# Turned attention weights: from an image in DRAM to sixteen transfers a unit within SBUF

## The chip, the cores and the metric

The kernel runs on one core of a Trainium2 chip. The metric is device time in microseconds, the median of several runs. The profile comes from one further execution, taken by the hardware profiler; its engines are TensorE (PE, with PEld for weight loads), VectorE (DVE), ScalarE (ACT), GpSimd (POOL) and SyncE (SP), which issues nearly all DMA transfers here.

## The reference

One transformer block with adaptive layer norm, in float32, for 8 sequences of 1024 tokens and width 512, 16 heads of 32:

```python
mod = jax.nn.silu(condition) @ Wada + bada
sh_a, sc_a, gt_a, sh_m, sc_m, gt_m = jnp.split(mod, 6, axis=1)
xm = _layernorm(x, g1, be1) * (1.0 + sc_a[:, None, :]) + sh_a[:, None, :]
x = x + gt_a[:, None, :] * _attention(xm, Wqkv, Wproj, bproj)
xm = _layernorm(x, g2, be2) * (1.0 + sc_m[:, None, :]) + sh_m[:, None, :]
h = jax.nn.gelu(xm @ W1 + b1, approximate=False)
x = x + gt_m[:, None, :] * (h @ W2 + b2)
```

`_attention` is causal: per head `softmax(where(causal, q @ k.T * 32 ** -0.5, -inf)) @ v`, then the output projection.

## The kernel before

The 8 sequences are cut into 16 blocks of 512 tokens; a sequence's first block (even number n) attends to itself only, its second (odd n) to both. Activations and weights stay in float32. The linear layers (k, q, v, output projection, up, down) go through `matmul` (line 217), four matmuls of 32 rows of output side by side; the square ones are cut into seven products instead of eight, from sums of weight quarters that a preparation leaves in DRAM. Weights come in pieces of 256 KB through a ring of eight SBUF buffers (`fetch`, lines 347 to 363; issues on lines 358, 360, 362): a piece is fetched when the piece eight before it is used up.

All instructions are written out in one order by a planner in the kernel's Python code. `note`, `note_pe` and `note_dma` keep a planned clock for each engine; generators ("threads") yield what they wait for, and `work` advances the one that is due first by that clock. The main thread is the linear work, window by window; the attention's loops put score and weight work between, at a pace (`pace`, `stream`), and side threads started with `start` handle smaller chains. On the chip each engine then works through its own list in order, SP too: an issue that waits holds back all issues behind it. Normalised tiles (`turn`, lines 723 and 728) also pass SP: written to DRAM (`held`) and read back turned (`hat`), and TensorE needs them for the linear layers (`xm_a`, `xm_m`).

Attention works in groups g of four heads (128 of the 512 columns). For the odd blocks and block 0, scores are computed twice, once to find row maxima (line 1613), once transposed (line 1721), so that the exponentials come out with keys in partitions, as the product with v needs them. The other even blocks, n = 2, 4, ..., 14, seven of them, are attended "by rows" (`attend_rows`). There the scores are computed once, with query rows in partitions, in ten units a block (`row_units`, `rows_unit`). A unit takes:

- a page, one of three SBUF buffers of 128 x 2048 (`free_p`, `take_slot`, `give_slot`), at most two of them raw pages at a time (`raws`);
- matmuls into the one score bank `st` (line 2021), a mask (2028), row maxima (2032), and exponentials by ScalarE into the raw page, with the sums accumulated (line 2040);
- one transpose of 32 x 32 squares by VectorE in place (line 2053).

What remains is to bring the squares to their mirrored partitions. Before the change this passes DRAM: `scatter` (line 2068) writes each part of the page into an image, `gather` reads a group's finished image back as three pages of up to eight squares by two key blocks (line 2143), and the products with v run over up to 256 columns at a time into the one bank `po` (line 2155):

```python
(both, 0, 0, 2), (both, 1, 1, 2)                        # page 0 of a group
(both, 0, 2, 2), (second, 1, 3, 3), (first, 1, 1, 1)    # page 1
(both, 0, 0, 0),                                        # page 2
```

Each entry gives the query columns, the place in the page, the key block and the first query block. As long as a block still has units to issue, one page of turned weights is held at a time (`pages`, `PAGE`). `inverses` turns the row sums' reciprocals into a tile of rows through a small DRAM tile (lines 2097 and 2105), and `finish_rows` multiplies the bank with it (line 2183, or 2179 and a multiply). The following odd block's first product waits in the plan until all four groups are `gathered` (line 1925).

## Time and profile before

| | us |
|---|---|
| median of 3 runs | 3542.0 |
| lowest, highest | 3541.5, 3550.18 |
| the profiled execution | 3545.22 |
| its span, first to last instruction | 3543.5 |
| TensorE busy in it | 3377.7 |
| VectorE busy | 2339.5 |
| ScalarE busy | 1248.8 |
| GpSimd busy | 1762.9 |

The DMA engines moved 645.42 MB, 506.31 MB of it read from HBM and 129.27 MB written, counted by the instructions. A busy share is a mean over stages with different limits; the stages attended by rows begin at 416, 818, 1252, 1682, 2111, 2535 and 2963 us. In groups of instructions a line ends with busy time, the mean of one in ns, and the engine's idle time before them with what ended it. A product of the program appears as two matmul instructions.

### The profile page before, as it was taken

The page shows a single profiled execution, that of the slowest core. Times are in us where ns is not written, and L with a number is a line of the kernel's source. Part 1 is how long each engine was busy: PE and PEld are TensorE (multiplying, and loading weights), DVE is VectorE, ACT ScalarE, POOL GpSimd, SP SyncE. Part 2 cuts the span into 40 slices and gives each one's busy share as a digit, 9 for nine tenths or more (in the row PEclk, how much of TensorE's full clock was granted, in tenths as well). Part 3 has the DMA queues.
Part 4 walks back from the last instruction along what each step waited for, and adds up shares of the span by engine and source line. Part 5 has one row for each costly group of instructions (what it writes and reads, how often), then busy time and mean ns, then how long its engine had stood idle before and what let it go on. Part 6 is the DMA issues. An engine that isn't in the chain of part 4 may idle for free.

```text
span 3543.5 us, 118795 instructions
## 1 busy us (share of the span) xinstructions
PE 3377.7 (95%) x52861; PEld 1705.4 (48%) x52861; DVE 2339.5 (66%) x2562; ACT 1248.8 (35%) x1970; POOL 1762.9 (50%) x1710
## 2 busy tenths in 40 slices
PE   8999889999899998999999999999999999899999
PEld 4444445444454444544454454544555445454455
DVE  5766577657577575775767757676677667566563
ACT  2334333343233532335223353333523334232521
POOL 3667713756037650477405674066731667208640
PEclk9999999999999999999999999999999999999999
DMA  6843487537875378753886538865498555973344
GB/s 198 263 148 112 150 235 214 155 109 213 245 209 155 102 226 239 209 153 103 247 233 189 153 109 264 253 185 142 127 284 236 147 142 154 284 221 111 92 135 138
DMA packets 502579, 645.42 MB, mean 182 GB/s; under 512 B 40365, under 2 KB 334061, under 8 KB 498485
## 3 DMA queue, kind: packets, MB, share of 16 engines
q1 hardware_dynamic: 501952, 637.80, 60.8%
q8 instruction: 416, 6.82, 0.8%
q14 instruction: 95, 0.77, 0.1%
q10 hardware_dynamic: 116, 0.03, 0.0%
HBM read 506.31 MB, written 129.27 MB: 179 GB/s over the span
## 4 chain that ended last, share of the span: by engine, by line
PE 37%; DMA 6%; POOL 4%; DVE 3%; issue 1%; SPq 1%; ACT 1%; DVEq 0%; POOLq 0%; ACTq 0%
PE bank L217 27%; PE sc L1613 3%; POOL pT L1856 3%; PE po L1762 2%; PE st L1721 2%; DMA held_m<-xm_m 1%; DMA turned<-image 1%; PE rows_sc L2021 1%; PE st L1709 1%; PE po L2155 1%; DVE mx L1628 1%; DMA w<-in_L_cond_Wproj_dram 1%; DMA hat_m<-held_m 1%; PE bank L1783 0%; DMA w<-in_L_cond_W_dram 0%
## 5 line engine op out<-in xcount | busy, mean ns | idle before, releaser
L1856 POOL TENSOR_TENSOR pT<-pT,pT 128x512 f32<-128x512 f32 (+3 forms) x918 | 981.9, 1104 | 250.5 <-ACT pT L1734 197.2
L217 PE MATMUL bank<-w,hT 128*32 128x256 f32 x14336 | 822.4, 380 | 0.9 <-ACT y_d L204 0.9
L1734 ACT ACTIVATE pT<-st 128x2048 f32<-128x2048 f32 x218 | 409.5, 1879 | 762.1 <-PE st L1721 573.9
L217 PEld LDWEIGHTS bank<-w,hT 128*32 128x32 f32 x14336 | 457.0, 110 | 372.7 <-issue 87.5
L1628 DVE TENSOR_REDUCE mx<-sc 128x4 f32<-128x2048 f32 (+3 forms) x271 | 499.4, 1859 | 183.0 <-PE sc L1613 179.7
L217 PE MATMUL bank<-xm_m,w 128*32 128x256 f32 x8192 | 506.6, 384 | 28.8 <-DMA w<-in_L_cond_W_dram 19.7
L2040 ACT ACTIVATE rows_p<-rows_sc,rows_minus 128x256 f32<-128x256 f32 (+3 forms) x448 | 229.6, 534 | 448.0 <-DVE rows_minus L2034 246.4
L217 PE MATMUL bank<-t_m,w 128*32 128x256 f32 x6144 | 382.9, 380 | 1.1 <-DVE hT L208 0.9
L217 PEld LDWEIGHTS bank<-xm_m,w 128*32 128x32 f32 x8192 | 257.8, 111 | 245.5 <-issue 66.4
L217 PEld LDWEIGHTS bank<-t_m,w 128*32 128x32 f32 x6144 | 190.7, 110 | 179.8 <-issue 58.3
L217 PE MATMUL bank<-xm_a,w 128*32 128x256 f32 x3968 | 252.1, 392 | 26.0 <-DVE xm_a L782 16.3
L217 PE MATMUL bank<-w,qT 128*32 128x512 f32 x2048 | 242.0, 610 | 16.3 <-DMA w<-in_L_cond_Wproj_dram 16.2
L1613 PE MATMUL sc<-kT,qT 32*128 32x512 f32 (+3 forms) x2168 | 250.6, 546 | 6.9 <-DVE mx L1628 3.5
L1762 PE MATMUL po<-pT,v 128*32 128x512 f32 (+3 forms) x2176 | 232.0, 515 | 4.5 <-POOL pT L1739 4.4
L1721 PE MATMUL st<-qT,kT 32*128 32x512 f32 (+3 forms) x2176 | 228.5, 508 | 0.0
L208 DVE TENSOR_TENSOR hT<-bank,u_u 128x512 f32<-128x512 f32 x181 | 121.4, 683 | 113.0 <-PE bank L217 110.6
L217 PEld LDWEIGHTS bank<-xm_a,w 128*32 128x32 f32 x3968 | 131.7, 113 | 131.3 <-issue 29.2
L217 PE MATMUL bank<-t_a,w 128*32 128x256 f32 x2944 | 184.4, 383 | 2.6 <-DVE qT L208 2.1
L2053 DVE STREAM_TRANSPOSE rows_p<-rows_p 128x2048 f32<-128x2048 f32 x70 | 160.9, 2298 | 36.2 <-ACT rows_p L2040 35.5
L1625 DVE TENSOR_TENSOR sc<-sc,mask 128x1024 f32<-128x1024 f32 (+1 forms) x89 | 90.5, 1017 | 124.4 <-PE sc L1613 91.9
L1129 ACT ACTIVATE hT<-hT,cols 128x512 f32<-128x512 f32 x256 | 164.4, 711 | 22.8 <-DVE hT L208 21.6
L655 POOL TENSOR_SCALAR rstd_a<-mv_a 128x4 f32<-128x4 f32 x14 | 3.2, 231 | 333.6 <-DVE mv_a L634 333.1
(268 smaller groups left out, 4152.9 us busy)
## 6 DMA issues: line engine op xcount, KB each, us to landing
w<-in_L_cond_W_dram SPq DMA_DIRECT2D x384, 256.0 KB
w<-kept_up_S SPq DMA_DIRECT2D x256, 256.0 KB
w<-kept_down_S SPq DMA_DIRECT2D x256, 256.0 KB
w<-kept_qkv_S SPq DMA_DIRECT2D x180, 256.0 KB
w<-in_L_cond_Wqkv_dram SPq DMA_DIRECT2D x147, 256.0 KB
image<-rows_p SPq DMA_DIRECT2D x112, 256.0 KB
turned<-image SPq DMA_DIRECT2D x28, 1024.0 KB
turned<-image SPq DMA_DIRECT2D x56, 512.0 KB
```

What stands on the lines that cost most here:

```text
L208: nc.vector.tensor_tensor(out, src, other, op)
L217: nc.tensor.matmul(ps[r, :], columns, rhs, start=start, stop=stop, skip_group_check=True)
L1129: nc.scalar.activation(hT[:, i, :], hT[:, i, :], AF.Gelu, bias=cols[:, O_B1 + f : O_B1 + f + 1])
L1613: nc.tensor.matmul(sc[:, j, c0 : c0 + w], qTs[n][r, gg, ts(qt, P)], keys_of(n, kh)[r, gg, :w], start=True, stop=True, skip_group_check=True,)
L1625: nc.vector.tensor_tensor(place, place, shape_of.to_broadcast(place.shape), ALU.add)
L1628: nc.vector.tensor_reduce(maxima[n, gg][:, kh, qt, :], sc[:, :, c0 : c0 + w], axis=AX.X, op=ALU.max)
L1721: nc.tensor.matmul(st[:, j, c0 : c0 + w], kT[r, gg, ts(k % NTT, P)], qT[r, gg, TB - w :], start=False, stop=True, skip_group_check=True,)
L1734: nc.scalar.activation(pT[:, :, :used], st[:, :, :used], AF.Exp, scale=scale)
L1762: nc.tensor.matmul(po[r, TB - w :], v[:, k % NTT, g * P + j * hd : g * P + (j + 1) * hd], pT[:, j, c0 : c0 + w], start=(k == 0), stop=last ...
L1856: nc.gpsimd.tensor_tensor(into, into, pT[:, j, c0 : c0 + w], ALU.add)
L2040: nc.scalar.activation(tile_of[:, j], sc[:, j, c0 : c0 + w].rearrange("p (k b x) -> p k b x", b=NTT, x=hd), AF.Exp, bias=minus[:, i, j : j ...
L2053: nc.vector.transpose(raw, raw)
```

## The change

The image, its writes and its reads go. When a unit's raw page has been transposed, a thread `spread_unit` takes a second page, and sixteen transfers, one for each pair of partition quarters a and b, move 32 partitions of 512 contiguous elements (64 KB) from the raw page into it; then the raw page is free again. The products with v run from this page over one key block and 128 query columns at a time. Pages are taken in the order of the units, and each unit's products follow those of the unit before. The raw page's columns are laid out in four runs of 512 instead of part by part; the units of a group come in the order of the score units. `finish_rows` no longer waits for the inverses: without them it copies the bank out with ScalarE and multiplies in a thread later. The planned cost of a transfer, and two allowances (1500 and 2500 ns), are new.

```diff
-    SLOT, PAGE = "a page", "a page to turned rows"
-    all_issued, pages = [True], []
+    SLOT = "a page"
...
-            todo += [(g, parts) for parts in mine[2:] + mine[:2]]
+            todo += [(g, parts) for parts in mine]
+        for i, (g, parts) in enumerate(todo):
+            order_of[n, g, parts[0][0]] = i
+            written["paged", n, i] = written["valued rows", n, i] = NEVER
+        written["paged", n, -1] = 0.0
...
-        places, at = [], 0
+        runs = raw.rearrange("p (b r) -> p b r", b=NTT)
         for i, (qt, kh, c0, w, gg) in enumerate(parts):
-            tile_of = raw[:, at : at + HPG * w].rearrange("p (b k j x) -> p j k b x", b=NTT, j=HPG, x=hd)
+            tile_of = runs[:, :, c0 : c0 + w].rearrange("p b (k j x) -> p j k b x", j=HPG, x=hd)
...
             nc.vector.transpose(raw, raw)
             note("DVE", 2320, [("p", slot)], [("p", slot)])
-            start(scatter())
-
-        def scatter():
-            yield [("p", slot)], []
-            for qt, w, gg, at in places:
-                count = w // P
...
-                for a in range(NTT):
-                    into = images[n, gg][qt // 2][:, qt % 2, a, :count, :]
-                    nc.sync.dma_start(
-                        into.rearrange("(b k) s e -> k b (s e)", k=hd),
-                        raw[ts(a, hd), at : at + HPG * w].rearrange("k (b f) -> k b f", b=NTT),
+            written["p", slot] += 1500
+            start(spread_unit(n, raw, slot, parts, order_of[n, g, parts[0][0]]))
...
+    def spread_unit(n, raw, slot, parts, i):
+        while True:
+            yield [("p", slot), SLOT, ("paged", n, i - 1)], []
+            if free_p:
+                break
+        taken_slot = take_slot()
+        key = ("p", taken_slot)
+        yield [("p", slot)], [key]
+        written["paged", n, i] = 0.0
+        page = pp.tile([P, NTT, TB], F32, tag=f"p{taken_slot}", name=f"turned_{n}_{i}")
+        for a in range(NTT):
+            for b in range(NTT):
+                nc.sync.dma_start(page[ts(b, hd), a, :], raw[ts(a, hd), ts(b, TB)])
+                note_dma(190, [("p", slot)], [key])
+        written[key] += 2500
+        left["p", slot] = now["DMA"] + LAND
+        raws.remove(slot)
+        give_slot(slot)
+        if i:
+            yield [("valued rows", n, i - 1)], []
+        for qt, kh, c0, w, gg in parts:
+            first = (n, gg) not in row_outs
+            for k in range(w // P):
+                yield [key, ("v", n), ("v done", n)], ["po"] if first and k == 0 else []
...
+                for j in range(HPG):
+                    r = slice(j * hd, (j + 1) * hd)
+                    at = c0 + k * P + j * hd
+                    nc.tensor.matmul(
+                        out[0][r, ts(qt, P)],
+                        vs[n][:, k, gg * P + j * hd : gg * P + (j + 1) * hd],
+                        page[:, :, at : at + hd],
...
+                note_pe(2 * COLUMN * P, "columns", [key], ["po"])
+            if out[1] == 10:
+                finish_rows(n, gg, out[0])
+        give_slot(taken_slot)
+        written["valued rows", n, i] = 0.0
...
-    def gather(n, g):
...
-            for at, source, ns in moves[i]:
-                nc.sync.dma_start(page[(slice(None), *at)], source)
-                note_dma(ns, [], [key])
-            written[key] += LATE
...
-                    nc.tensor.matmul(
-                        state["out"][r, qt * P : qt * P + wide],
-                        vs[n][:, k, g * P + j * hd : g * P + (j + 1) * hd],
-                        page[:, rows_of, at, r],
...
-            if state["left"] == 0:
-                yield [("inverses", n, g), "po"], []
-                finish_rows(n, g, state["out"])
...
     def finish_rows(n, g, out):
-        key, into, by = ("att", n), qTs[n][:, g, :], inverse_rows.pop((n, g))
-        ready = due(["top", "po"])
-        if max(now["DVE"], ready) > max(now["ACT"], ready) + 2500:
+        into = qTs[n][:, g, :]
+        if wait_of(([("inverses", n, g)], [])) > 0 or max(now["DVE"], due(["po"])) > max(now["ACT"], due(["po"])) + 2500:
             nc.scalar.copy(into, out)
-            note_act(585, None, ["po"], [key])
-            either(into, into, by, ALU.mult, ["top"], [key])
+            note_act(585, None, ["po"], [("values", n, g)])
+            start(scaled(n, g, into))
         else:
-            nc.vector.tensor_tensor(into, out, by, ALU.mult)
+            nc.vector.tensor_tensor(into, out, inverse_rows.pop((n, g)), ALU.mult)
...
+    def scaled(n, g, into):
+        yield [("inverses", n, g), ("values", n, g)], []
+        either(into, into, inverse_rows.pop((n, g)), ALU.mult, ["top"], [("att", n)])
+        finished(n, g)
```

89 lines of the change are left out of this document (13 added, 76 removed).

## The prediction

> **What bounds the kernel now.** I read the page first (engine totals, DMA queue), then the table of stretches over the stages in which seven of the sixteen blocks are attended by rows, the only ones that the change touches. After those came what TensorE waits for, SP's own waits, and the groups and lines that carry the durations.
>
> ```profile
> span 3543.5 us, 118795 instructions
> ...
> PE 3377.7 (95%) x52861; PEld 1705.4 (48%) x52861; DVE 2339.5 (66%) x2562; ACT 1248.8 (35%) x1970; POOL 1762.9 (50%) x1710
> ```
>
> TensorE is busy for 95%, so all its idle time together is 166 us, and no change beside it can win much more than that. The first seven lines below run each from the first row score of such a block to its last product; the eighth is the stage of a block done the other way.
>
> ```profile
> core 0: us, PE busy (x) PEld busy (x) DVE busy (x) ACT busy (x) POOL busy (x), PEclk, DMA share, GB/s
> 416.00:582.00 166.00, 140.30 (x2092) 69.50 (x2088) 127.06 (x141) 61.17 (x165) 25.91 (x32) 0.93 0.81 234
> 818.00:1030.00 212.00, 194.41 (x3192) 104.99 (x3192) 151.66 (x171) 69.15 (x176) 56.40 (x53) 0.98 0.84 243
> 1252.00:1467.00 215.00, 199.08 (x3276) 106.98 (x3276) 152.73 (x172) 68.24 (x176) 57.20 (x53) 0.97 0.83 246
> 1682.00:1896.00 214.00, 200.24 (x3272) 108.85 (x3276) 147.89 (x171) 70.94 (x180) 58.37 (x55) 0.97 0.84 248
> 2111.00:2327.00 216.00, 205.00 (x3400) 112.67 (x3400) 157.75 (x176) 74.39 (x183) 59.39 (x52) 0.98 0.83 251
> 2535.00:2752.00 217.00, 203.53 (x3384) 111.25 (x3378) 158.05 (x177) 72.07 (x181) 59.79 (x53) 0.98 0.84 250
> 2963.00:3185.00 222.00, 207.47 (x3467) 115.25 (x3467) 154.38 (x169) 70.64 (x177) 58.46 (x49) 0.98 0.82 243
> 1467.00:1682.00 215.00, 212.50 (x3164) 98.94 (x3157) 143.06 (x148) 84.19 (x79) 159.20 (x151) 1.00 0.46 131
> ```
>
> Width less TensorE's busy time: 25.7, 17.6, 15.9, 13.8, 11.0, 13.5, 14.5, together 112 of the 166 us, against 2.5 us in the eighth line. The DMA engines are busy for 0.81 to 0.84 there and for 0.46 in the other stage, and TensorE's granted clock stands at 0.93 to 0.98 instead of 1.00. So the rows stages lose their time where DMA is dense. TensorE's waits name the transfers:
>
> ```profile
> PE bank L217 <- DMA w<-in_L_cond_W_dram: 19.7, 3, 7.5
> PE po L2155 <- DMA turned<-image: 17.1, 19, 3.2
> PE bank L217 <- DVE xm_a L782: 16.3, 2, 8.6
> PE bank L217 <- DMA w<-in_L_cond_Wproj_dram: 16.2, 11, 4.5
> PE rows_sc L2021 <- ACT rows_p L2040: 12.5, 4, 7.9
> ```
>
> These five make 81.8 us, asked stage by stage practically all of it inside the seven. Only the second is the image's own landing; the first and fourth are weights that come late, the third a normalised tile that comes back late from DRAM, the fifth ScalarE holding the single score bank.
>
> **The change, part by part.** It removes the image: writes at line 2068, reads at 2143. It adds sixteen transfers of 64 KB a unit (32 partitions of 2 KB), all on SP's queue.
>
> *DMA bytes.* A group of four heads has ten blocks of 128x128 by four heads, 2.6 MB written and as much read; a block has four groups, 21 MB a stage. The third line has 246 GB/s for 215 us, 53 MB. Afterwards each unit moves 1.05 MB once, 10.5 MB a stage: 42 MB, and in that proportion the DMA share falls from 0.83 to about 0.67.
>
> *SP's issues.* From the views of the source lines, with min/median/max ns: the two removed kinds, the row nearest to the new transfer (32 partitions of 2 KB, 64 KB), and the count of units:
>
> ```profile
> L2068 SPq DMA_DIRECT2D image<-rows_p x448: 302/448/2548, 427.9 to 3167.8; - x150
> L2143 SPq DMA_DIRECT2D turned<-image x140: 359/548/3066, 454.2 to 3174.6; - x140
> ```
> ```profile
> L2105 SPq DMA_DIRECT2D inverse<-inverse_rows x112: 302/413/2577, 455.5 to 3184.4; - x112
> ```
> ```profile
> L2053 DVE STREAM_TRANSPOSE rows_p<-rows_p x70: 2247/2302/2314, 425.6 to 3159.1; 128x2048 f32<-128x2048 f32 x70
> ```
>
> There are 70 units, so 1120 issues replace 588. At the medians: 1120 x 0.413 = 463 us against 448 x 0.448 + 140 x 0.548 = 277, or 27 us more of SP in each of seven stages. SP's slack there is the time in which it waits for TensorE to free a weight buffer; SP's waits in 1252 to 1467 us:
>
> ```profile
> SPq L358 <- PE bank L217: 27.0, 19, 4.0
> SPq L360 <- PE bank L217: 23.9, 19, 2.6
> ```
>
> 51 us, so the 27 fit on average and cost nothing; if the cover were gone, they would be 27 x 7 = 187 us in the extreme. As a burst they matter more: sixteen issues at 0.413 are 6.6 us in which no weight is fetched. Weights queue behind on SP, also the normalised tiles' moves, and TensorE waits for both.
>
> Here a rule speaks against the change. The Trainium skill, SBUF — State Buffer, section on the DMA setup-cost knee, says that a loop of 64 KiB transfers reaches only some 138 GB/s and that one should coalesce. As an estimate from that page a unit's megabyte would take 7.6 us; the issue row gives 6.6, so the trace agrees on the size. Were the difference of 1 us exposed in all 70 units, the sum would come out 30 us slower instead of 40 faster.
>
> *TensorE.* The same columns, but in moving tiles of 128 instead of mostly 256. Each product shows as two instructions: 896 of 256 columns and 448 of 128 become 2240 of 128.
>
> ```profile
> L2155 PE MATMUL po<-turned,v 128*32 128x256 f32 x896 | 67.9, 395 | 17.1 <-DMA turned<-image 16.8
> ...
> L2155 PE MATMUL po<-turned,v 128*32 128x128 f32 x448 | 19.2, 280 | 0.3 <-DMA turned<-image 0.3
> ```
> ```profile
> 1326.02 0.64 PE L2155 MATMUL po<-turned,v 128*32 128x256 f32 x8 [0.50 <-DMA turned<-image]
> ...
> 1327.66 0.64 PE L2155 MATMUL po<-turned,v 128*32 128x128 f32 x16
> ```
> ```profile
> L2155 PEldq EVENT_SEMAPHORE  x40: 51/51/51, 461.3 to 3182.1; - x40
> ```
>
> In the time line sixteen of 128 take as long as eight of 256, 0.64 us: no cost. By the groups, 2240 x 42.9 ns = 96 us against 87: 9 us. I take 5. The first product on a page must now wait for sixteen landings, not one to three. No row shows that. It is bounded by nothing (another wait was passed already) and by sixteen waits of 51 ns, 0.8 us a unit, 57 us. Four waits a unit, half of them hidden behind running products, are 7 us; I take that, nearer to the lower end because the present pages with up to three landings show so few queue waits (40 for 84 pages).
>
> *Others.* ScalarE's 448 exponentials and VectorE's 70 transposes stay. A group that is ready before its inverses is copied out by ScalarE and multiplied later: ScalarE at 35% hides it, and the bank comes free sooner. With that cover gone it is one more operation for each of 28 groups, 19 us by the multiply of today:
>
> ```profile
> L2183 DVE TENSOR_TENSOR qT<-po,inverse 128x512 f32<-128x512 f32 x20 | 13.6, 682 | 30.3 <-DMA inverse<-inverse_rows 27.6 <-DMA w<-in_L_cond_Wqkv_dram 1.9 <-PE po L2155 0.7
> ```
>
>  The order of units and the wait of each unit for the one before cost nothing while there is linear work to put between; the two-hop path through DRAM is gone.
>
> *The waits.* Of the 81.8 us I take half as recovered, 41: the queue is a fifth emptier, but part of the stalls come from order on SP, which longer bursts can renew. A new page can be late as the old one was (17.1 us for 84 pages, 0.2 each); that is inside the half not recovered. The clock: about 1350 us of busy time at 0.975 lie some 33 us above full clock; a third back, 11.
>
> Sum: 41 + 11 won, 5 + 7 spent: 40 us faster. The profiled execution took 3545.2 us (span 3543.5), 3.2 above the median of the runs, 3542.0. So 3505 on its own scale, **3502** on the median's.
>
> **The rivals.**
>
> *The burst starves the weights (slower).* This is how SP's order costs TensorE today:
>
> ```profile
> 2654.43 2.74 SPq L728 DMA_DIRECT2D hat_m<-held_m  x4
> 2657.21 1.65 SPq L2143 DMA_DIRECT2D turned<-image  x3
> 2659.18 3.32 SPq L2105 DMA_DIRECT2D inverse<-inverse_rows  x4
> 2663.46 1.62 SPq L358 DMA_DIRECT2D w<-in_L_cond_W_dram  x2
> ```
> ```profile
> 2669.27 1.08 PE L217 MATMUL bank<-xm_m,w 128*32 128x256 f32 x8 [6.96 <-DMA w<-in_L_cond_W_dram]
> ```
>
> Eleven issues hold SP for 9 us, then the weight takes 5.8 us from issue to product, and TensorE stands for 7. In the dense stage eight image writes took 6.64 us, in the quiet start 3.76:
>
> ```profile
> 1334.13 6.64 SPq L2068 DMA_DIRECT2D image<-rows_p  x8
> ```
> ```profile
> 427.90 3.76 SPq L2068 DMA_DIRECT2D image<-rows_p  x8
> ```
> ```profile
> 2653.47 1.94 PE L217 MATMUL bank<-xm_a,w 128*32 128x256 f32 x32
> 2655.19 1.94 PE L217 MATMUL bank<-t_a,w 128*32 128x256 f32 x32
> ```
>
> A weight buffer lasts 1.72 us (the distance of the last two lines), eight of them 13.8 us. A burst of sixteen plus 5.8 us for the next weight exceeds that from a pace of 0.50 us an issue on. The quiet pace (0.47) stays just below, the dense one (0.83) gives 13.3 + 5.8 - 13.8 = 5.3 us of stall. If a quarter of the 70 bursts meet that, 93 us, less the 40: 53 slower, **3595**. For it: the pace of today. [...] Against: the pace was measured with the queue at 0.83, and TensorE also does row and score work that uses no weights.
>
> *The pages hold the score bank (slower).* Three page buffers now serve a raw page and a turned page for each unit, and an exponential into a page must wait for sixteen landings out of it. Today ScalarE waits long but seldom (12.5 us of it reach TensorE). At 1 us a unit reaching TensorE, 70, less half of the forecast's gain lost with it: about 30 slower, **3572**.
>
> *Only the place of the wait changes.* The late weights and tiles come from SP's order, not from the image's bytes; TensorE's idle time stays at about 112 us: **3542**.
>
> **How the numbers follow.** Forecast 0.48, its own range 3440 (all of the 81.8 and the 33 of the clock, less the 12) to 3530; the burst 0.34; the page buffers 0.10; no change 0.08. Nothing under 0.3% (about 10 us) can be told from no change. The range reaches from 3440 to 3615, three in ten of the bursts stalling. Faster 0.48, same 0.08, slower 0.44.
>
> **What would show it.** Right: in the seven stages the DMA share at 0.65 to 0.70, TensorE's idle time near 70 us instead of 112, the clock nearer to 1.00, 1120 issues at about 0.41 us, HBM traffic lower by some 73 MB each way. Wrong by the burst: waits of TensorE on `w` longer than before, each behind a run of sixteen issues slower than 0.5 us. Wrong by the pages: waits for the new page, or of ScalarE's exponentials for DMA, above 0.5 us a unit. Wrong on TensorE: more busy time than 12 us above today's at the same clock.

## The result, and the profile after

The changed kernel takes 3748.02 us (median of 4 runs, 3734.43 to 3751.36) against 3544.84 for the kernel before: a ratio of 1.0564, interval 1.0533 to 1.0596. That is 203 us slower, where 40 us faster was forecast, and beyond the range's upper end of 3615. The profiled execution took 3751.36.

The page after, in the lines that answer to those of before:

```profile
span 3749.6 us, 121347 instructions
...
PE 3435.7 (92%) x53757; PEld 1772.6 (47%) x53757; DVE 2347.0 (63%) x2564; ACT 1251.4 (33%) x1968; POOL 1749.9 (47%) x1708
...
DMA packets 389247, 572.23 MB, mean 153 GB/s; under 512 B 48876, under 2 KB 199212, under 8 KB 385140
...
HBM read 432.91 MB, written 55.87 MB: 130 GB/s over the span
...
PE 62%; SPq 14%; DMA 11%; POOL 5%; DVE 4%; issue 3%; ACT 2%; DVEq 0%; ACTq 0%; POOLq 0%
PE bank L217 42%; SPq L2066 12%; PE sc L1613 5%; PE po L1760 4%; PE st L1719 4%; POOL pT L1854 4%; DMA turned<-rows_p 2%; PE po L2085 2%; PE st L1707 1%; DMA w<-kept_up_S 1%; DMA hat_m<-held_m 1%; PE bank L1781 1%; DMA w<-kept_qkv_S 1%; DMA
```

The last two lines are the chain that ended last, in shares of the span. SP's queue holds 14% of it, nearly all by line 2066, the sixteen transfers. Before the change it held 1%, though the chain told there covers only about half of the span:

```profile
PE 37%; DMA 6%; POOL 4%; DVE 3%; issue 1%; SPq 1%; ACT 1%; DVEq 0%; POOLq 0%; ACTq 0%
```

HBM traffic fell by 73 MB each way, from 506.31 and 129.27. The same stages in the table of stretches, the eighth line again a block done the other way:

```profile
core 0: us, PE busy (x) PEld busy (x) DVE busy (x) ACT busy (x) POOL busy (x), PEclk, DMA share, GB/s
417.00:612.00 195.00, 155.94 (x2412) 83.70 (x2408) 132.81 (x142) 64.42 (x170) 29.04 (x33) 0.89 0.55 153
838.00:1049.00 211.00, 175.75 (x2877) 103.73 (x2881) 143.33 (x163) 53.01 (x156) 47.53 (x43) 0.92 0.64 178
1294.00:1522.00 228.00, 193.11 (x3168) 108.75 (x3168) 144.49 (x164) 66.43 (x174) 52.20 (x47) 0.93 0.64 176
1754.00:1990.00 236.00, 208.03 (x3504) 121.18 (x3500) 151.46 (x177) 65.50 (x172) 48.73 (x45) 0.96 0.65 182
2212.00:2448.00 236.00, 198.52 (x3272) 113.88 (x3268) 148.36 (x167) 67.14 (x175) 52.35 (x46) 0.93 0.62 174
2671.00:2920.00 249.00, 209.30 (x3384) 118.61 (x3380) 157.69 (x175) 72.38 (x181) 52.67 (x45) 0.92 0.60 170
3142.00:3388.00 246.00, 208.56 (x3424) 120.41 (x3424) 153.59 (x167) 70.76 (x179) 51.40 (x44) 0.94 0.59 168
1522.00:1754.00 232.00, 227.31 (x3400) 107.07 (x3392) 144.19 (x145) 92.89 (x89) 162.43 (x163) 0.99 0.44 132
```

The DMA share is down to between 0.55 and 0.65. Yet width less TensorE's busy time is 39.1, 35.3, 34.9, 28.0, 37.5, 39.7 and 37.4, together 252 us against 112. The account of the span (3749.6 against 3543.5, 206 us): 140 from this idle time, 58 from TensorE's busy time (3435.7 against 3377.7), 8 from idle time elsewhere. By stages, the seven are 1601 us wide instead of 1462 and hold 938 fewer matmuls of the rest of the program; these follow in the stages between, which are 67 us longer. What TensorE waits for:

```profile
PE po L2085 <- DMA turned<-rows_p: 165.7, 48, 7.8
PE bank L217 <- DMA w<-in_L_cond_W_dram: 11.6, 2, 10.1
```

Waits on the new page alone are 165.7 us, where the old one was 17.1. One such wait, with the issues, SP's line and TensorE's lines from the time lines:

```profile
L2066 SPq DMA_DIRECT2D turned<-rows_p x1120: 507/589/2002, 429.0 to 3384.4; - x187
```
```profile
2775.56 11.07 SPq L2066 DMA_DIRECT2D turned<-rows_p  x16
```
```profile
2742.40 1.06 PE L2085 MATMUL po<-turned,v 128*32 128x128 f32 x32
...
2788.33 1.73 PE L2085 MATMUL po<-turned,v 128*32 128x128 f32 x32 [5.14 <-DMA turned<-rows_p]
```

An issue holds SP for 589 ns at the median. Sixteen of them take 11.07 us here (11.3 at the median over the 70 units), and the product begins 1.7 us after the last (1.8 at the median). That is 12.8 us after the first issue, with TensorE idle for 5.14 of them. The two lines of TensorE show the second cost as well: the same 32 matmuls take 1.73 us behind that gap and 1.06 without one. Matmuls that take over 1.25 times the median of their form fill 218 us of this trace and 98 of the one before. At 1.55 to 1.75 times their usual time (423 against 273 ns on line 2085, 3.38 against 1.93 us in run 4), the 120 us more of them are, as an estimate, 43 to 51 of the 58 us of busy time. The products' own group, the same columns, went from 87.1 to 100.2 us.

### The profile page after: what moved, and what is told of

It reads as the page before. It is cut to its first block, busy times and chain, and to the rows that moved or that the text cites. A ratio compares the mean times of both kernels' runs of the same rounds, so it can differ in the third digit from the quotient of the medians.

```text
span 3749.6 us, 121347 instructions
## 1 busy us (share of the span) xinstructions
PE 3435.7 (92%) x53757; PEld 1772.6 (47%) x53757; DVE 2347.0 (63%) x2564; ACT 1251.4 (33%) x1968; POOL 1749.9 (47%) x1708
## 4 chain that ended last, share of the span: by engine, by line
PE 62%; SPq 14%; DMA 11%; POOL 5%; DVE 4%; issue 3%; ACT 2%; DVEq 0%; ACTq 0%; POOLq 0%
PE bank L217 42%; SPq L2066 12%; PE sc L1613 5%; PE po L1760 4%; PE st L1719 4%; POOL pT L1854 4%; DMA turned<-rows_p 2%; PE po L2085 2%; PE st L1707 1%; DMA w<-kept_up_S 1%; DMA hat_m<-held_m 1%; PE bank L1781 1%; DMA w<-kept_qkv_S 1%; DMA w<-in_L_cond_W_dram 1%; PE rows_sc L2016 1%
## 5 line engine op out<-in xcount | busy, mean ns | idle before, releaser
L217 PE MATMUL bank<-xm_m,w 128*32 128x256 f32 x8192 | 517.3, 387 | 33.3 <-ACT xm_m L788 11.4
L2035 ACT ACTIVATE rows_p<-rows_sc,rows_minus 128x512 f32<-128x512 f32 (+3 forms) x448 | 229.6, 535 | 511.2 <-DVE rows_minus L2029 176.1
L217 PEld LDWEIGHTS bank<-t_m,w 128*32 128x32 f32 x6144 | 198.4, 112 | 173.9 <-issue 51.3
L2085 PE MATMUL po<-turned,v 128*32 128x128 f32 x2240 | 100.2, 325 | 172.7 <-DMA turned<-rows_p 165.7
L217 PE MATMUL bank<-t_a,w 128*32 128x256 f32 x2944 | 195.9, 399 | 3.6 <-DVE qT L208 1.9
L170 POOL TENSOR_TENSOR t_m<-t_m,xm_m 128x512 f32<-128x512 f32 x10 | 17.4, 1737 | 358.5 <-DVE t_m L800 358.5
```

What stands on the lines that cost most here:

```text
L217: nc.tensor.matmul(ps[r, :], columns, rhs, start=start, stop=stop, skip_group_check=True)
L2035: nc.scalar.activation(tile_of[:, j], sc[:, j, c0 : c0 + w].rearrange("p (k b x) -> p k b x", b=NTT, x=hd), AF.Exp, bias=minus[:, i, j : j ...
L2085: nc.tensor.matmul(out[0][r, ts(qt, P)], vs[n][:, k, gg * P + j * hd : gg * P + (j + 1) * hd], page[:, :, at : at + hd], start=out[1] == 1 ...
```

## The experiments

The letters of the theories belong to each run's own text. The main theory: SP is held by issues that are dearer than the prediction's row, so pages, and whatever stands behind them, come late. Its rivals: the bytes or the path within SBUF are slow; three page buffers are too few for the longer chain of a unit; the planner's wrong estimate is the cause; the rest of the change is.

**1. The price of an issue, by itself.** A small program on an idle queue: sixteen issues each of several kinds.

> Leaves out the whole computation and only issues transfers of several forms on an idle queue: sixteen of 64 KB within SBUF from one partition quarter to another, sixteen that stay in their quarter, sixteen of 64 KB over 128 partitions within SBUF, sixteen of 16 KB within SBUF, sixteen of 64 KB from SBUF to DRAM and from DRAM to SBUF, four of 256 KB within SBUF, a megabyte to DRAM, four turned reads of 256 KB, and the sixteen from ScalarE's queue. Theory A: a transfer within SBUF holds SP about 0.59 us whatever its bytes, one with a side in DRAM 0.30 to 0.42. If instead the queue's load made the 0.59, all of them take 0.30 to 0.42 here.

The rows of its source lines (min/median/max ns), in order: 64 KB between quarters within SBUF; SBUF to DRAM; DRAM to SBUF; 256 KB over 128 partitions within SBUF; the first again on ScalarE's queue:

```profile
L38 SPq DMA_DIRECT2D far<-raw x16: 588/604/788, 6.2 to 16.0; - x16
...
L46 SPq DMA_DIRECT2D mem<-raw x16: 303/423/577, 47.3 to 54.8; - x16
...
L48 SPq DMA_DIRECT2D far<-mem x16: 340/419/433, 55.2 to 62.2; - x16
...
L50 SPq DMA_DIRECT2D far<-raw x4: 521/604/607, 62.7 to 64.5; - x4
...
L60 ACTq DMA_DIRECT2D ex<-raw x16: 544/604/612, 6.2 to 15.8; - x16
```

An issue with both sides in SBUF costs 0.59 to 0.60 us at the median, with 16 KB (589), 64 KB or 256 KB, over 32 partitions or 128, on an idle queue as in the kernel. With one side in DRAM it is 0.42 at 64 KB. So in these rows the price follows where the two sides lie, and not the bytes. It is not the whole rule, as three other rows show, two of this program and one of the changed kernel:

```profile
L52 SPq DMA_DIRECT2D mem<-raw x4: 442/894/1234, 65.2 to 67.6; - x4
...
L54 SPq DMA_DIRECT2D far<-mem x4: 342/1230/1264, 69.8 to 72.7; - x4
```
```profile
L2112 SPq DMA_DIRECT2D inverse_rows<-inverse x28: 580/591/1202, 456.7 to 3385.7; - x28
```

The first are four writes of 1 MB to DRAM, the second four turned reads of 256 KB straight behind them, the third a write of 8 KB to DRAM in runs of 128 bytes. Turned reads of that form take 430 ns in run 5, where no such writes stand before them; why these three are dear stays open.

**2. Four issues instead of sixteen, the same bytes.** The squares stay on their partitions, the plan is that of the change.

```diff
         for a in range(NTT):
+            nc.sync.dma_start(page[:, a, :], raw[:, ts(a, TB)])
             for b in range(NTT):
-                nc.sync.dma_start(page[ts(b, hd), a, :], raw[ts(a, hd), ts(b, TB)])
                 note_dma(190, [("p", slot)], [key])
```

> Four transfers of 128 partitions (256 KB each) instead of sixteen of 32: the same bytes from the raw page to the turned page in the same place of the program, with the planner's account unchanged. The squares do not change their partitions, so the values are not the reference's. Theory A (issues): four issues of about 0.4 us, the page there some 4 us after the first, waits for the page under 20 us, time 3480 to 3560. Theory C (moving a megabyte within SBUF is slow by itself): waits for the page stay above 100 us, time above 3680. Theory B (page buffers): between, 3560 to 3650, as the chain is 9 us shorter.

3483.27 us, ratio 0.9828 (0.9808 to 0.9848): 62 us faster than the kernel before and 265 faster than the change. The burst is 2.6 us, and the largest waits are no longer the page's:

```profile
PE po L2085 <- DVE qT L2133: 13.1, 4, 4.2
PE rows_sc L2016 <- ACT rows_p L2035: 12.2, 3, 6.4
```

The seven stages in the table of stretches, columns as before:

```profile
414.00:582.00 168.00, 147.12 (x2412) 78.40 (x2408) 128.06 (x142) 63.88 (x169) 30.53 (x35) 0.96 0.58 189
808.00:991.00 183.00, 170.74 (x2895) 95.53 (x2892) 141.53 (x161) 53.12 (x157) 46.70 (x40) 0.96 0.68 211
1233.00:1418.00 185.00, 180.48 (x3167) 101.79 (x3160) 142.83 (x163) 65.81 (x173) 52.82 (x48) 1.00 0.71 224
1649.00:1855.00 206.00, 200.65 (x3512) 113.64 (x3512) 151.88 (x177) 65.77 (x173) 49.95 (x46) 0.99 0.68 214
2072.00:2267.00 195.00, 188.10 (x3272) 105.74 (x3272) 146.57 (x166) 67.07 (x175) 51.22 (x45) 0.99 0.69 218
2490.00:2694.00 204.00, 195.75 (x3388) 109.35 (x3384) 155.75 (x174) 72.42 (x181) 53.18 (x45) 0.98 0.67 212
2916.00:3117.00 201.00, 195.40 (x3404) 109.50 (x3400) 152.54 (x167) 70.32 (x178) 50.40 (x39) 0.99 0.66 210
```

Width less busy time is 64 us in all, not 112 or 252, and the clock is at 0.96 to 1.00. The squares do not change quarters here; in run 1, though, squares that do are issued and land much like those that do not (604 and 589 ns, landed 2.1 and 2.0 us after the issue's start). So neither the bytes nor the path is the cause, but the number of issues, and the gain that was forecast for the emptier queue exists. The run also shows what the plan allows: with nothing waiting for a page, a product begins 11.0 us after its unit's first issue, at the median. The change's sixteen issues and their landing need at least 11.8.

**3. Eight and twelve.** Eight transfers of 64 partitions, squares unmoved, plan unchanged; and, with the whole computation, twelve transfers, while GpSimd copies the four squares that stay on their partitions (planned at 640 ns a transfer).

```diff
+            for h in range(2):
+                nc.sync.dma_start(page[ts(h, 2 * hd), a, :], raw[ts(h, 2 * hd), ts(a, TB)])
```
```diff
+            nc.gpsimd.tensor_copy(page[ts(a, hd), a, :], raw[ts(a, hd), ts(a, TB)])
+            note("POOL", 800, [("p", slot)], [key])
...
+                if a != b:
+                    nc.sync.dma_start(page[ts(b, hd), a, :], raw[ts(a, hd), ts(b, TB)])
```

> Eight transfers of 64 partitions (128 KB) instead of sixteen, the same bytes, the planner's account unchanged, the squares not moved between partitions (the values are not the reference's). It asks how the time depends on the number of issues between four (3483 us) and sixteen (3748). Theory A1 (TensorE stands only for what the page comes later than the plan's 11.3 us from first issue to product): eight issues take 5.1 us, the page is there after some 8 to 9 us, so no wait, time 3475 to 3510. Theory A2 (every issue costs TensorE, as SP is short of time): halfway by count, about 3570.

> The four squares that stay in their partition quarter are copied by GpSimd (4 copies of 32 x 512 a unit); twelve transfers remain, accounted for with 640 ns each and no allowance beyond the landing, 9.4 us by plan from first issue to the page; everything is computed. From four and eight issues (3483 and 3517 us, 8.5 us an issue) the line gives 3551 at twelve if the page comes before the product; GpSimd's copies are about 3 us a unit on an engine that is idle for 158 of 215 us. Theory A1 (late against the plan is what costs): 3530 to 3570. If twelve issues already lie on the steep part (29 us an issue from eight to sixteen), 3630.

Eight: 3517.19 (0.9925, 0.9906 to 0.9945), 7 us above theory A1, with 12.5 us of waits on the page. Twelve: 3636.74 (1.0256, 1.0236 to 1.0277), 79.2 us of them: 67 us above the 3570 of its text, on the steep part already. From four to eight an issue more a unit costs 8.5 us in all (34 / 4), from eight to sixteen 29 (231 / 8). The cost is not linear: eight issues take 5.8 us at the median and still fit, with their landing, into the 11 us that the plan allows; sixteen do not. The twelve had a plan of their own and GpSimd's copies, so their place between is less sure.

**4. The plan corrected, with sixteen and with four.** The planner believes in 425 ns an issue. Here it gets 215 ns more for each, and 6000 instead of 2500 ns behind the last; then the same with the four transfers of run 2.

```diff
                 note_dma(190, [("p", slot)], [key])
-        written[key] += 2500
+                now["SP"] += 215
+        written[key] += 6000
```

> The sixteen transfers are kept; only the planner's account of them changes: 215 ns more of SP for each issue (640 instead of 425, as the trace has them) and 6000 instead of 2500 ns of allowance after the last one, so that the products are placed about 6.7 us later behind the issues. Theory A (the planner puts the products where the page cannot be yet, since an issue holds SP for 0.59 us and not 0.41, and TensorE stands in its fixed order): TensorE's waits for the page fall from 166 us to under 60, its clock in the rows stages goes up, time 3580 to 3650. Theory B (three page buffers: the chain raw page, sixteen transfers, products is too long for them, whatever the plan says): the waits only move to other places, time above 3700.

> The four large transfers of the second experiment (values not the reference's, as there) under the corrected account of the first one: the plan believes in sixteen issues of 640 ns and an allowance of 6000, the chip has the page after some 7 us. It asks why the corrected account did not help. Theory A (the chip's SP, held for 11 us a unit, made the weights late): with SP free the time is that of the four transfers, 3480 to 3540. Theory B (a unit's planned chain, 17 us from first issue to product with three pages, stretches the rows stages and uses up their linear work, whatever the chip does): rows stages of 240 us or more, time above 3600.

| | four issues | sixteen issues |
|---|---|---|
| the change's plan | 3483.27 | 3748.02 |
| corrected plan | 3525.14 (0.9946, 0.9929 to 0.9963) | 3709.81 (1.0465, 1.0439 to 1.0491) |

Correcting the plan wins 38 us with sixteen issues and costs 42 with four. Under one plan the twelve more issues cost 265 or 185. So this correction wins back a fifth of the loss; since it makes the kernel with four issues slower, another might win more; with sixteen issues in one run, none was tried. 3709.81 is also where theory B of its text put it, that three page buffers are too few for a long chain. But four issues under the same plan, with the same buffers and a product 18.2 us after the first issue at the median, take 3525.14, as theory A of that text has it: the long planned chain alone does not cost the loss. What TensorE waits for changes with the plan; after the correction, sixteen issues:

```profile
PE bank L217 <- DMA w<-in_L_cond_W_dram: 40.3, 20, 4.5
PE bank L217 <- DMA w<-kept_up_S: 34.3, 9, 6.2
...
PE po L2086 <- DMA turned<-rows_p: 15.8, 5, 8.2
```

The page falls from 165.7 to 15.8 us, and waits on weights appear in its place (98.5 us with `kept_qkv`, 13.1, and `kept_down`, 10.8). Its time lines of SP and of TensorE show how:

```profile
1365.95 11.66 SPq L2066 DMA_DIRECT2D turned<-rows_p  x16
1377.66 2.03 SPq L360 DMA_DIRECT2D w<-kept_qkv_S  x4
```
```profile
1380.84 3.38 PE L217 MATMUL bank<-w,t_a 128*32 128x256 f32 x32 [3.39 <-DMA w<-kept_qkv_S]
...
1408.11 1.93 PE L217 MATMUL bank<-xm_a,w 128*32 128x256 f32 x32
...
1430.26 1.93 PE L217 MATMUL bank<-t_m,w 128*32 128x256 f32 x32 [2.59 <-DMA w<-in_L_cond_W_dram]
```

The first weight behind the burst is issued when it ends and is used 3.2 us later; TensorE, out of weights, stood for 3.39.

**5. Another path, and bursts in parts.** One write of 1 MB to DRAM and four turned reads of 256 KB; and four runs of four issues with linear work between, under a corrected plan with an allowance of 4000 ns.

```diff
+        nc.sync.dma_start(held, raw)
...
+        for b in range(NTT):
+            nc.sync.dma_start(page[ts(b, hd), :, :], held[:, ts(b, TB)].rearrange("(a k) f -> k a f", k=hd))
```
```diff
+            if a < NTT - 1:
+                written["part", n, i, a] = max(now["SP"], now["PE"] + 2600)
+                yield [("part", n, i, a)], []
```

> Another way to the same turned page, with five issues: the raw page goes to DRAM whole (1 MB, runs of 8 KB), and four transfers of 256 KB (runs of 2 KB) bring it back turned. The raw page is given back after one issue, the turned page is taken only when the first hop has landed by plan. Theory A (issues): SP gives about 2.2 us a unit, waits for the page under 40 us, time 3500 to 3580. Theory B (page buffers): the chain is as long as with sixteen transfers, two hops of 5 us or more, time above 3650. Theory C (bytes within SBUF): the path through DRAM has none of them, time near the kernel before or below.

> All sixteen transfers on SP, but in four runs of four with linear work, and so weight fetches, let in between (at least 2.6 us by plan), and with the planner's account as in the first experiment (640 ns an issue, allowance 4000). The longest hold of SP falls from 11.3 to 2.6 us, the sum of the issues stays, the chain of a unit gets longer. Theory A (the run of sixteen is what hurts: late page by the old plan, late weights by the corrected one): waits for weights fall from about 100 us in the first experiment to under 40, time 3560 to 3640. Theory B (the chain of a unit is too long for three pages): no better than the first experiment, 3700 or more.

Through DRAM: 3656.92 (1.0313, 1.0298 to 1.0329), with 104.6 us of waits on the page. That is far above theory A and just inside theory B, a chain as long as with sixteen transfers. Five issues hold SP for a short time only, but a product begins 10 us after the first read's issue, and TensorE waits for it. So late pages cost a lot even where SP is not held. In parts: 3727.1 (1.0529, 1.0501 to 1.0558), as theory B of its text. Most of the waits on weights go, as meant; 41.4 us on the page stay, and 82 us of waits on VectorE's row maxima come. Spreading the burst wins nothing against the 3709.81 of the corrected plan.

**6. Other queues.** Half of the transfers on ScalarE's queue, or on GpSimd's; and with twelve transfers (four squares copied by GpSimd) six on SP and six on GpSimd's queue.

```diff
+                queue = nc.scalar if b % 2 else nc.sync
+                queue.dma_start(page[ts(b, hd), a, :], raw[ts(a, hd), ts(b, TB)])
```
```diff
+                queue = nc.gpsimd if b % 2 else nc.sync
```
```diff
+                    queue = nc.gpsimd if at_queue % 2 else nc.sync
```

> Eight of the sixteen transfers go out from ScalarE's queue, eight from SP's, both accounted for in the plan (600 ns each on ScalarE). All bytes, squares and pages as in the change. Theory A: SP's run is 5.1 us, the page comes some 7.5 us after the first issue, waits for the page under 40 us, late weights few; ScalarE pays 8 x 0.6 x 70 = 336 us of a time that is two thirds idle, some of which comes back as late exponentials and bank copies: 3500 to 3600. Theory B: the chain gets 5 us shorter, a third of the way to the four transfers, 3660.

> As before this one, with GpSimd's queue in place of ScalarE's for eight of the sixteen (1000 ns each in the plan). GpSimd is busy for 57 of 215 us in the rows stages and nothing of ScalarE is held up. Theory A: if an issue there takes no longer than about 1 us, as with ScalarE or better, 3490 to 3580; if GpSimd is slower at it, the page is late again and the time is between this and the change's.

> Whole computation. The four squares on the diagonal, which stay where they are, are copied by GpSimd (about 0.6 us each, from the run with twelve transfers); of the other twelve transfers six go out on SP's queue and six on GpSimd's, in turn. Theory A (what counts is how long one queue is held: 6 x 0.63 = 3.8 us on SP, 4 x 0.6 + 6 x 0.5 = 5.4 us on GpSimd): between four and eight transfers on SP, 3500 to 3560 us, no slower than the kernel before by over half a per cent. Theory B (GpSimd's issues wait for landings of transfers eight before, as with eight and eight, which took 3599): 3570 to 3610, with page waits above 40 us.

3701.26 (1.0444, 1.0422 to 1.0465), 3599.15 (1.0163, 1.0135 to 1.0192) and 3603.96 (1.0166, 1.0142 to 1.0189). The first lies above both its theories, the second 19 us above its theory A. ScalarE is held for 602 ns an issue, GpSimd for 496. In the trace SP's and ScalarE's transfers count their landings on the same eight semaphores, so in the first run an issue on one queue can wait for the landing of a transfer of the other, a weight among them. GpSimd's count on eight of their own. The profile still puts long waits of GpSimd in the second run down to weights, but its time lines show what ended them:

```profile
POOL turned L2067 <- DMA w<-kept_up_S: 56.7, 6, 13.6
POOL turned L2067 <- DMA w<-in_L_cond_W_dram: 54.7, 6, 14.3
```
```profile
523.71 2.31 DVE L2046 STREAM_TRANSPOSE rows_p<-rows_p 128x2048 f32<-128x2048 f32 x1
...
526.32 3.90 POOL L2067 DMA_DIRECT2D turned<-rows_p  x8 [12.56 <-DMA w<-in_L_cond_W_dram]
```

GpSimd begins 0.3 us after the unit's transposition ends. The first of its eight issues waits for up to eighteen semaphores, and the profile names the one that changed last. In 29 of the 30 units in which that is a weight's, the issue begins within 0.6 us of the end of the transposition or of one of TensorE's products on a page, so the weight is not what it waited for. GpSimd's first issue is also ahead of SP's in 49 of the 70 units: it is not GpSimd's queue that makes the page late. The third run, with six issues on each, is no better than the second, and its waits on the page are 88.1 us. Time and waits are those of theory B of its text, but its reason, the landings of transfers eight before, is not borne out; what holds these pages up stays open.

The Trainium skill, DMA: Bandwidth & Descriptors, section "Issuing engines are not separate DMA queues", says that starting transfers from several engines saves only the sequencer's time, "which is usually small relative to the DMA itself". The first half fits: the second run, with eight issues less on SP and its own plan, is 149 us faster than the change. The second half does not hold here: sixteen issues hold the sequencer for 11.3 us, and the product begins 1.8 us after the last.

**7. The rest of the change alone.** The image in DRAM, its writes and reads as before; the plain order of the units and the later multiply stay.

```diff
-            todo += [(g, parts) for parts in mine[2:] + mine[:2]]
+            todo += [(g, parts) for parts in mine]
...
-                yield [("inverses", n, g), "po"], []
```

> The sixteen transfers undone: pages go to DRAM as an image and come back turned, as in the kernel before; what else the change brought stays (units in plain order, and a group's rows copied out by ScalarE and multiplied later where the inverses are late). Theory A (the time is lost by the sixteen issues alone): near the kernel before, 3530 to 3560 us, and no wait of TensorE on a page above 30 us. Theory B (the order of units or the late multiply costs a good part of the 203 us): 3600 us or more, with TensorE waiting for the rows stages' other links (score bank, inverses, pages).

3565.15 (1.0058, 1.0037 to 1.0079): 5 us above the upper end of theory A, with 25.2 us of waits on the page. Beside the image, the rest is not free, as was assumed, but costs about 20 us; it is not the cause of the 203.

**8. No transfers: is it SP, or the lateness?** GpSimd copies all sixteen squares; then eight, SP moving the other eight at the same time.

```diff
-                nc.sync.dma_start(page[ts(b, hd), a, :], raw[ts(a, hd), ts(b, TB)])
-                note_dma(190, [("p", slot)], [key])
-        written[key] += 2500
+                nc.gpsimd.tensor_copy(page[ts(b, hd), a, :], raw[ts(a, hd), ts(b, TB)])
+                note("POOL", 640, [("p", slot)], [key])
```

> Whole computation, no transfer of squares: GpSimd copies all sixteen squares of a unit between partitions (601/609 ns each for the ones on the diagonal in the run with twelve transfers, so 9.7 us a unit, 680 us in all, planned at 640 ns each). SP is free of 1120 issues, the page is complete about 10 us after its transposition, much as late as with the sixteen transfers. Theory A (SP being held is what costs): no late weights, DMA share lower still, 3450 to 3560 us. Theory B (the lateness of the page costs, whoever moves it, or GpSimd's other work is now late): 3600 us or more, with waits on the page or on GpSimd's tiles in the seven stages.

> Whole computation: eight squares as transfers on SP (8 x 0.63 = 5.0 us), the other eight copied by GpSimd at the same time (8 x 0.61 = 4.9 us, 340 us of GpSimd in all). If only the length of the longer of the two counts, the run with eight transfers (3517 us) is met: 3505 to 3540 us. If GpSimd's own work is made late by it (it is busy for 57 of 215 us in these stages), 3570 or more, with TensorE waiting for GpSimd.

All by GpSimd: 3599.23 (1.015, 1.0133 to 1.0167), just below where theory B begins. No weight stands among the larger waits, but the page does, complete 10.4 us after the first copy (the median):

```profile
PE po L2084 <- POOL turned L2066: 64.3, 34, 9.6
```

This plan knew the copies' length. Against sixteen issues under a plan that knew theirs (3709.81), freeing SP, and having the page some 3 us sooner, is worth 111 us; against four issues (3525.14, where the plan reserves the time of sixteen), a page that is late by itself, and GpSimd's load, cost 74. So both the held SP and the late page hold a part of the loss; how much each, no run divides cleanly, since the plans differ as well. Half and half: 3561.93 (1.005, 1.0035 to 1.0065), between its two expectations, with 38.5 us of waits on the page and 14.4 on a small tile (`mcols`) that GpSimd makes.

**9. Divided among more engines.** The first six or eight squares as transfers, the others as copies:

| transfers on SP | copies | us | ratio, interval |
|---|---|---|---|
| 6 | 6 GpSimd, 4 ScalarE | 3606.13 | 1.0171, 1.0156 to 1.0186 |
| 6 | 6 GpSimd, 4 VectorE | 3582.61 | 1.0114, 1.0087 to 1.0142 |
| 8 | 4 GpSimd, 4 VectorE | 3623.37 | 1.0233, 1.0206 to 1.026 |
| 8 | 8 VectorE | 3659.9 | 1.0336, 1.0312 to 1.036 |

```diff
+        for a, b in squares[6:12]:
+            nc.gpsimd.tensor_copy(page[ts(b, hd), a, :], raw[ts(a, hd), ts(b, TB)])
+            note("POOL", 640, [("p", slot)], [key])
+        for a, b in squares[12:]:
+            nc.scalar.copy(page[ts(b, hd), a, :], raw[ts(a, hd), ts(b, TB)])
+            note_act(585, None, [("p", slot)], [key])
```

> Whole computation: six squares as transfers on SP (6 x 0.63 = 3.8 us), six copied by GpSimd (3.7 us), four by ScalarE (585 ns each in the plan, 2.3 us). By the line from four transfers (3483) to eight (3517) six are worth 3500; the copies lie beside. Theory A (the longest of the three counts): 3485 to 3525 us, faster than the kernel before by 0.5 to 1.7%. Theory B (ScalarE, whose exponentials stand at the head of each unit's chain, and GpSimd pay for their copies): 3545 or more, with waits on row scores or GpSimd's tiles.

> Whole computation: eight squares as transfers on SP (5.0 us), eight copied by VectorE, which transposed them just before (planned at 400 ns each, no row has the form; 128x512 out of a bank takes it 680). VectorE is busy for 152 of 215 us in these stages. If a copy takes 0.4 us (3.2 us a unit, 32 us a stage): 3500 to 3540 us. If it takes 0.6 (48 a stage, 93% busy): 3560 or more, with TensorE waiting for VectorE.

> Whole computation: eight squares as transfers on SP (5.0 us), four copied by GpSimd (2.4 us), four by VectorE. Both engines keep room, so the nearest to the run with eight transfers alone (3517): 3505 to 3545 us. If even so it lies at 3560 or above, neither the copying engine's load nor its time explains the difference between 3517 and 3562.

> Whole computation: six transfers on SP (3.8 us), six copies on GpSimd (3.7 us), four on VectorE. As the run with ScalarE in place of VectorE (3606), which planned the same lengths: if ScalarE's copies were what made that one slow, 3500 to 3550 us; if not, 3580 or more again.

All four lie above the hopes of their texts. The copies themselves are short (610 ns on GpSimd, 615 on ScalarE, 420 on VectorE), and waits on the page are down to some 15 to 40 us. VectorE in ScalarE's place is 24 us better, so ScalarE's copies were not the main cost. With eight copies on VectorE two of its own results come late, 28.4 and 20.1 us:

```profile
PE bank L217 <- DVE xm_m L782: 28.4, 3, 10.9
...
PE st L1707 <- DVE mx L1628: 20.1, 12, 6.6
```

Why 8 and 8 on VectorE (3660) is worse than on GpSimd (3562), though the plan and the length of a copy (400 and 420 ns) agree, stays open. Four copies on each, where both engines keep room, take 3623, which by that run's own text speaks against the engines' load. The versions also differ in which squares are copied (every other one in the 3562, the last ones of the page in the 3660), and no run took that, or the new order in which the planner then puts the rest, apart. No version with the whole computation beat the kernel before; the nearest are 3561.93 and, with the image, 3565.15.

## Why the prediction was wrong

**The step that failed is "SP's issues".** It took the row nearest in bytes and partitions, 64 KB over 32 partitions at 0.413 us, but that row has one side in DRAM. The form of the change costs 0.589 at the median and 0.637 in the mean; with the time between issues a burst is 11.3 us, not 6.6. The profile before had two issues with both sides in SBUF, of 1 MB each, and they were dearer than the row taken:

```profile
L1045 SPq DMA_DIRECT2D v<-v_early x1: 548/548/548, 422.6 to 422.6; - x1
```
```profile
L1036 SPq DMA_DIRECT2D kT<-kT_early x1: 483/483/483, 435.0 to 435.0; - x1
```

That its 6.6 us lay near the estimate of 7.6 says nothing of this form. At medians SP is held for 1120 x 0.589 = 660 us against the 277 before, 55 us more in each stage, not 27; by the sums in the traces it is 713 against 376, 48 more. "Fit on average" held all the same. In the changed kernel SP still waits 29 us for TensorE to free weight buffers in the stage from 1294 us, and 51 and 47 in those from 1754 and 2671, though TensorE itself stands more there:

```profile
SPq L360 <- PE bank L217: 19.4, 13, 3.6
SPq L358 <- PE bank L217: 9.8, 8, 2.5
```

"Cost nothing" is what failed. Not the mean but the single burst costs: run 3 shows that eight issues are nearly hidden and sixteen are not.

**The second step that failed is the lateness of the new page.** It stood "inside the half not recovered", as the old page's 0.2 us, beside 0.1 for the queue waits of its sixteen landings. It was 2.4 us a unit (165.7 / 70), since the product follows the first issue by 13.3 us at the median, where the plan allows 11.0; "the two-hop path through DRAM is gone" was right and worth less than the sixteen issues took. Run 8 suggests that a page that takes 10 us costs a good part of this even where SP is free. The queue waits themselves were sized rightly: 253 on line 2085, 3.6 a unit, most of 51 ns, against the four that were taken.

**The rival of the burst** had the right mechanism in the wrong place. It asked for a pace above 0.50 us an issue and had 0.59 to meet it. In the changed kernel its sign is nearly absent, though: waits on weights are fewer than before, and TensorE stands for the page instead. With the plan corrected they appear as it described, 3.39 us at the place shown beside its 5.3. That they make 98.5 us beside its 93 is luck: these are 40 waits of 2.5 us, not a quarter of 70 bursts at 5.3. Its total, 3595, set against that the forecast's gain.

**The rival of the pages.** Its sign, "waits for the new page, or of ScalarE's exponentials for DMA, above 0.5 us a unit", came true in both halves: 2.4 us for the page, and ScalarE's exponentials stand 163.3 us for the sixteen transfers, 2.3 a unit:

```profile
ACT rows_p L2035 <- DMA turned<-rows_p: 163.3, 14, 24.1
```

But its way to TensorE, the score bank held by ScalarE, did not: that wait is 9.6 us now, 12.5 before. Its sum does not come out either: 70 less half of the gain is 50, and its 30 takes the whole gain off. (In the same way the 27 x 7 of SP's issues is 189, not 187.)

**What was right.** HBM traffic fell by the 73 MB each way, the DMA share to 0.55 to 0.65 (0.67 was forecast), and the gain did lie there: with the same bytes and four issues the DMA share is 0.66 to 0.71 in the last six stages, these lose 64 us with the first (70 was forecast), and the kernel takes 3483, inside the forecast's own range. The products in tiles of 128 columns, for which 5 us were set aside, cost nothing there: their group takes 80.2 us against 87.1. So the 100.2 in the changed kernel comes from the slow stretches and not from their form. "Only the place of the wait changes" falls by the same run.

**The clock** went the other way. A third of 33 us was to come back; instead it lies at 0.89 to 0.96 in the seven stages, against 0.93 to 0.98. The longer gaps go with it: in the lines of run 4 and of the result, 32 matmuls take 1.75 and 1.63 times as long behind gaps of 3.39 and 5.14 us, and the usual time behind one of 2.59. Over the whole trace of the change, most matmuls of the next 1.5 us take over 1.25 times the median of their form behind 34 of the 36 gaps of 3.4 us and more, behind 5 of 19 between 2 and 3.4, and behind 4 of 81 between 0.3 and 2. The Trainium skill, TensorE: Matmul & The Clock Gate, section on the HAM clock gate, has half the rate after an idle window of some 3.4 us; the trace agrees on the window, and shows 1.55 to 1.75 times the time. Waits above 3.4 us are thus paid in part once more, in busy time.

**Others.** The order of units and the later multiply, costed at nothing, are some 20 us together (run 7); which of the two was not tried apart.

## What to carry to other kernels

Cost a transfer's issue by a row of its own form, with its source and destination in the same memories, even a row of a single issue, and not by the one with its bytes. Where there is none, a small program such as run 1 gives it. Then multiply it by the burst and set that against the time that the plan leaves before the first use: a slack that is sufficient as a mean over a stage says nothing of the one burst. Before a wait is put down to the transfer that the profile names, look in the time line for what ended just before it. When a plan is written out ahead, try a new cost under a plan that knows it too, since the same delay shows as a late page under one and as late weights under the other.

## What the runs showed of the hardware

- A transfer within SBUF holds SP for 0.59 to 0.60 us an issue at the median, whether of 16, 64 or 256 KB, on 32 or 128 partitions; two single ones of 1 MB took 0.55 and 0.48 before the change. One with a side in DRAM holds it for 0.42 at 64 KB, but for 0.59 when it writes 8 KB in runs of 128 bytes, and for 0.89 and 1.23 in run 1's writes of 1 MB and the turned reads behind them. ScalarE is held for 0.60 on its own queue, GpSimd for 0.50 on its own.
- GpSimd, ScalarE and VectorE copy 32 x 512 elements of float32 from one partition quarter to another in 610, 615 and 420 ns.
- TensorE runs slower behind 34 of 36 gaps of 3.4 us and more, and behind 4 of 81 of 0.3 to 2 us, in the trace of the change.
- In these programs SP's and ScalarE's transfers share the eight semaphores of their landings, so that an issue can wait for a landing of the other queue; GpSimd's have eight of their own (run 6).
